# A message-passing layer on one core: blocks 26 to 103 go singly in TensorE's order, sums are placed later, and a softmax rests four turns

## Chip, core and metric

One core of a Trainium2 chip. The metric is the device time of one execution in microseconds: 1315.15 us for the kernel before, the median of three runs (1313.95 to 1321.31).

## What is computed

A graph layer over 8192 nodes with 256 features and 131072 edges sorted by destination, all in float32. `bn` is a scale and a shift per feature. The layer:

```
ea  = edge_attr @ w_e + b_e                       # 64 -> 256 features per edge
msg = relu(x[src] + ea)
agg = segment_sum(msg, dst)                       # over the edges of a node
h_local = bn(relu((x + agg) @ w1 + b1) @ w2 + b2 + x)
# attention inside groups of 32 consecutive nodes, 4 heads of 64
q, k, v = split(x @ in_w.T + in_b)
o = softmax(q k^T / 8) v
h_attn = bn(o @ out_w.T + out_b + x)
out = h_local + h_attn
out = bn(out + relu(out @ m_w1 + m_b1) @ m_w2 + m_b2)
result = layernorm(x + out)
```

## The kernel before

Two kinds of work share the core. **Edge work** goes over 128 blocks of 1024 edges. **Node work** goes over 16 chunks of 512 nodes (attention, then the dense layers once the chunk's sums are complete).

One block of edges takes these steps. The names are those of the profile; L numbers are lines of the kernel before.

- `gather(b)` (L152 to 163): eight indirect DMAs on GpSimd's queue fetch x rows of 128 edges each into a tile `xs`, of which there are four buffers. Blocks 0 to 19 read x itself, later ones `xb`, a copy of x with the edge bias added, which the kernel writes during the first blocks (`copy_load`, `copy_stream`, `copy_some`: loads and stores on SyncE's queue, adds on VectorE, L621).
- `load_edges`, `edge_transpose`, joined in `next_edges`: SyncE loads edge features, VectorE transposes them (L190).
- `edge_products(b)`: TensorE multiplies them by w_e (L208) into two PSUM tiles `pe`. For blocks under 20 it also adds the bias by a matmul (L203).
- `edge_messages(b)`: VectorE adds `xs` (L229, two adds a block), which frees the block's `xs` buffer; ScalarE applies the relu (L233).
- `edge_hot(b)`: VectorE builds a 0/1 matrix `oh` that sends each edge to one of 32 rows (L241).
- `edge_sums(blocks)`: TensorE multiplies it by the messages (L255) into one PSUM bank `pw`; ScalarE copies this to `ws` (L265); VectorE builds a second 0/1 matrix `oh2` (L269). It takes one block or two.
- `edge_place(blocks, ws, oh2)`: TensorE multiplies `ws` by `oh2` (L280), in the same bank under the name `l2`, and VectorE adds the window to the chunk's transposed nodes `xT` (L289).

Node work is written as generators that yield the planned cost, in microseconds, of the TensorE work that they have just issued. `attention_front` loads and transposes x (L434) and makes q and k (L445); `attention_back` makes v (L459) and the scores (L476, in the tiles `pe`), the softmax, its product with v (L514) and the output projection (L526); `dense` holds the four dense layers (L545), a transpose back (L582), the norm and the store. Four streams (BACK, FRONT, DENSE, DENSE2) hold these generators. `Work.run(us)` (L651) takes steps from the streams in turn until the planned costs reach `us`. A call of `run` is a turn: a generator that yields `REST` goes on in the second turn after the one in which it stopped, one that yields `PAUSE` in the next. If no stream may go, the rest of the amount is dropped down to 2 us.

The order on TensorE is the order of the program, written out by hand. On VectorE and ScalarE it is also stated for blocks below `NV` = 26 (`stated[0]`), and set by a scheduler of the language after that. Three parts follow each other in the main loop:

- blocks 0 to 103 (`TAIL` = 104), in pairs (L739 to 779). A pair issues, in this order: both gathers (two blocks ahead), products and messages of b, the sums of the pair before, products and messages of b + 1, the placing of those sums, and node work in three or four calls of `run` between these, `per` in all: 2 x 4.2 us for blocks under 20, 2 x 5.1 us later. Below 26 the calls are 0.3, then the place, 0.2 and 0.5; from 26 on they are 0.2, 0.1, then the place, 0.2, the `edge_hot` of both blocks, 0.5.
- blocks 104 to 127 (L781 to 825): a planner with a clock of its own takes the next step by due times. `came` holds the planned arrival of each block's gather, `added` that of its messages, and `work.step` fills the time until the next due step with node work.
- `work.finish()`, whatever is left.

Of the kernel before, what the change touches and what calls it, by code (L numbers as in the profile page):

```python
# [40 lines left out]
NV = 26  # L41
TAIL = 104
# [4 lines left out]
REST = -1.0  # L47
# [13 lines left out]
def first_node(b):  # L61
    return b * NPB - SLACK[b]
# [10 lines left out]
def gnn_kernel(ctx: ExitStack, tc: tile.TileContext, x, src, dst, edge_attr, w, out):  # L73
# [78 lines left out]
    def gather(b):  # L152
        xs = epool.tile([P, NH, TJ, C], FP, name="xs", tag="xs", bufs=4)
        for h in range(NH):
            for j in range(TJ):
                idx = srcd[:, b * NH + h, j : j + 1] if b < ND else srci[:, b, h * TJ + j : h * TJ + j + 1]
                nc.gpsimd.indirect_dma_start(  # L157
                    out=xs[:, h, j, :],
                    out_offset=None,
                    in_=x if b < NX else xb[:, :],  # L160
                    in_offset=bass.IndirectOffsetOnAxis(ap=idx, axis=0),
                )
        xs_of[b] = xs
# [19 lines left out]
    def between():  # L183
        for do in spots:
            do()
# [27 lines left out]
    def next_edges(b):  # L213
        if b < NB:
            edge_transpose(b)
        if b + 2 < NB:
            load_edges(b + 2)
# [18 lines left out]
    def edge_hot(b):  # L236

        oh = oh_of[b] = epool.tile([P, TB, WN], FP, name="oh", tag="oh", bufs=2)
        for t0 in range(0, TB, TB // 2):
            ts = slice(t0, t0 + TB // 2)  # L240
            nc.vector.tensor_tensor(  # L241
                oh[:, ts],
                iota_n[:, None, :WN].to_broadcast([P, TB // 2, WN]),
                rel[:, b, ts, None].to_broadcast([P, TB // 2, WN]),
                ALU.is_equal,
            )
# [45 lines left out]
    stated = [True]  # L292
# [336 lines left out]
    def copy_some(n=1):  # L629
        for _ in range(n):  # L630
            next(copying[0], None)

    class Work:
# [17 lines left out]
        def run(self, us):  # L651
            self.owed += us
            n = len(self.streams)
            self.rest = [max(r - 1, 0) for r in self.rest]
            while self.owed > 0:
                turns = [i % n for i in range(self.turn, self.turn + n)]
                i = next((i for i in turns if self.may(i)), None)
                if i is None:
                    break
                t = next(self.streams[i][0][1], None)  # L660
                if t is None:
                    self.streams[i].pop(0)
                elif t in (REST, PAUSE):
                    self.rest[i] = 2 if t == REST else 1
                else:
                    self.owed -= t
                    self.turn = (i + 1) % n
                    if t > 0:
                        between()
            self.owed = min(self.owed, 2.0)  # L670
# [24 lines left out]
    work = Work(4)  # L695
    PER = 5.1
    PER_X = 4.2
    OTHER = ("vn", "qk", "oT", "pr", "o")
    placed = -1
    with tc.manual_schedule(engines={PE}):  # L700

        def last_of(c, t_z=TN):

            return max(b for b in range(NB) if first_node(b) < c * CH + t_z * P)

        def summed(c, t_z=TN):
            last = last_of(c, t_z)
            return lambda: placed >= last and chunk[c].get("done") and not xp_of and b > 2

        for c in range(NCH):  # L710
            st, before, same = chunk[c], chunk[c - 1], chunk[c - 4]
            front = attention_front(c * CH, st, npool, bank)
            if c < 2:
                next(front)
            work.add(
                FRONT,
                lambda c=c, b=before, s=same: (c < 1 or b.get("scores"))
                and (c < 4 or s.get("dense")),
                front,
            )  # L720
            work.add(BACK, lambda s=st: s.get("front"), attention_back(st, npool, bank, bank2))
            if c < NCH - 2:
                work.add(DENSE, summed(c), dense(c * CH, st, npool, bank))
        for i, c, t_a, t_z in (
            (DENSE2, NCH - 2, 0, 2), (DENSE, NCH - 2, 2, 4), (DENSE2, NCH - 1, 0, 2), (DENSE, NCH - 1, 2, 3),
            (DENSE2, NCH - 1, 3, 4),
        ):
            d = dense(c * CH, chunk[c], npool, bank, t_a, t_z, *([OTHER] if i == DENSE2 else []))
            ready = summed(c, t_z)
            if i == DENSE2:  # L730
                ready = lambda r=ready: r() and chunk[NCH - 1].get("done")
            work.add(i, ready, d)

        spots.append(copy_some)
        early = ExitStack()
        early.enter_context(tc.manual_schedule(engines={mybir.EngineType.DVE, mybir.EngineType.Activation}))
        sums, waiting = None, []
        b = 0
        while b < TAIL:  # L739
            if b == NV:  # L740
                early.close()
                stated[0] = False
            blocks, per = range(b, b + 2), 2 * (PER_X if b < NX else PER)
            copying[0] = copy_stream(b // 2 - 1)
            for i in blocks:
                if i + 2 < NB:
                    gather(i + 2)
                if 4 <= i < 8:
                    wt, name = ((w1, "w1"), (w2, "w2"), (mw1, "m_w1"), (mw2, "m_w2"))[i - 4]
                    nc.sync.dma_start(wt, w[name].rearrange("(k p) m -> p k m", p=P))  # L750

            if b:
                edge_products(b)
                edge_messages(b)
                next_edges(b + 2)
            if waiting:
                sums = edge_sums(waiting)
            waiting = list(blocks)
            if not stated[0]:
                work.run(0.2 * per)  # L760
            edge_products(b + 1)
            edge_messages(b + 1)
            next_edges(b + 3)
            if stated[0]:
                for i in blocks:
                    edge_hot(i)
                    copy_some(2)
            work.run((0.3 if stated[0] else 0.1) * per)
            copy_load(b // 2)
            if sums:  # L770
                edge_place(*sums)
                placed, sums = sums[0][-1], None
            work.run(0.2 * per)
            if not stated[0]:
                for i in blocks:
                    edge_hot(i)
            work.run(0.5 * per)
            copy_some(4 * TN)
            b += 2

        came = [7.9 + 10.035 * (i + 1) for i in range(NB)]  # L781
        t, p, m, s, l = came[b - 2] + 20, b, b, b - 2, b - 2
        added = dict((i, came[i] + 2.0) for i in range(b))
        summed_at, bank_free = {}, t
        work.at = [t] * len(work.streams)
        while l < NB:

            times = [1e9] * 4
            if l < s:
                times[0] = summed_at[l] + 1.5  # L790
            elif s < m:
                times[1] = max(added[s] + 1.2, bank_free)
            if p < NB and m == p:
                times[2] = added[p - 1]
            if m < p:
                times[3] = came[m]
            if t >= times[0]:
                edge_place(*sums)
                placed = l
                t += 0.75  # L800
                bank_free = work.placed_at = t + 0.7
                l += 1
            elif t >= times[1]:
                sums = edge_sums([s])
                t += 1.2
                summed_at[s] = t
                s += 1
            elif t >= times[2]:
                if p + 2 < NB:
                    gather(p + 2)  # L810
                edge_products(p)
                next_edges(p + 2)
                edge_hot(p)
                t += 2.1
                p += 1
            elif t >= times[3]:

                with ExitStack() as behind:
                    for i in newest.values():
                        behind.enter_context(tc.issue_after(i))  # L820
                    edge_messages(m)
                added[m] = max(t, came[m], added[m - 1] + 0.5) + 2.0
                m += 1
            elif l == s - 1 == NB - 1:
                t = times[0]
            else:
                t = work.step(t, min(times))
        work.finish()
# [124 lines left out]
```

## Time and profile before

| | us |
|---|---|
| median of three runs | 1315.15 |
| the profiled execution, its own time | 1315.3 |
| span of its profile | 1313.3 |
| TensorE's matmuls busy | 1196.5 (91%) |
| GpSimd busy | 976.1 (74%) |
| VectorE busy | 800.9 (61%) |
| ScalarE busy | 589.2 (45%) |

Busy times are shares of one span and do not add up, as the engines work side by side. PE is TensorE's matmuls, PEld its weight loads, DVE VectorE, ACT ScalarE, POOL GpSimd, SP SyncE; a q behind the name is the engine's queue. A row with "x864 | 820.7, 950 | 263.4 <-issue 245.1" reads: 864 instructions, busy 820.7 us in all, 950 ns each, and 263.4 us in which the engine was idle just before them, 245.1 of it with no cause that the profile shows ("issue"). A row of a stretch gives its bounds, its length, each engine's busy time with the number of instructions, the granted TensorE clock (1 is full), the share of time in which the DMA engines were busy, and GB/s. A row of the chain or of the timeline begins with the start and the length in us.

### The profile page before, as it was taken

What the parts mean: (1) busy time and instruction counts of PE and PEld (TensorE: products, weight loads), DVE (VectorE), ACT (ScalarE), POOL (GpSimd) and SP (SyncE); (2) the same over time, 40 slices, a digit from 0 to 9 for tenths busy, and PEclk for the clock granted to TensorE, in tenths of its full rate; (3) what the DMA queues carried; (4) which work ended last, traced back from release to release, by engine and by line L of the source; (5) the groups of instructions that cost most, each with busy time, mean ns of one, the idle gap of its engine ahead of it and who ended that gap; (6) DMA issues with size and microseconds to landing.
All of it is one profiled execution on the core that took longest, in us unless ns stands there. A gap on an engine that the chain in (4) does not pass through costs nothing.

```text
span 1313.3 us, 20960 instructions
## 1 busy us (share of the span) xinstructions
PE 1196.5 (91%) x7635; PEld 720.4 (55%) x7635; DVE 800.9 (61%) x1629; ACT 589.2 (45%) x841; POOL 976.1 (74%) x1032
## 2 busy tenths in 40 slices
PE   4987989999999989898997998989898999989987
PEld 3554655556555655554554554545556555555655
DVE  5567665756666565745646574565647558475754
ACT  2524443454545363544544444353454445444433
POOL 6777777777777777777777777777777777777772
PEclk8988999999999989998998998989898999999989
DMA  9999876677766665755757566576567567655742
GB/s 234 283 338 273 263 210 175 172 183 193 177 170 170 169 183 162 195 155 157 194 157 185 154 185 168 154 186 170 170 169 189 149 169 193 162 162 161 193 129 58
DMA packets 148905, 240.34 MB, mean 183 GB/s; under 512 B 27934, under 2 KB 112188, under 8 KB 148028
## 3 DMA queue, kind: packets, MB, share of 16 engines
q0 software_dynamic: 49152, 134.28, 38.0%
q1 hardware_dynamic: 98556, 104.65, 29.5%
q8 instruction: 62, 1.02, 0.3%
q14 instruction: 47, 0.39, 0.1%
q10 hardware_dynamic: 1088, 0.00, 0.0%
HBM read 222.06 MB, written 16.78 MB: 182 GB/s over the span
## 4 chain that ended last, share of the span: by engine, by line
PE 49%; POOL 20%; issue 10%; DMA 9%; DVE 7%; ACT 4%; SPq 0%; DVEq 0%; POOLq 0%; ACTq 0%
POOL xs L157 20%; PE at L545 13%; PE pe L208 10%; PE at L445 6%; DMA xs<-xb,srci 5%; PE pw L255 5%; PE at L526 3%; PE l L280 3%; PE pe L203 2%; DVE msg L229 2%; PE at L459 2%; DMA xs<-in_x_dram,srci 2%; PE at L514 1%; ACT pr L486 1%; DVE bd L506 1%
## 5 line engine op out<-in xcount | busy, mean ns | idle before, releaser
L157 POOL DMA_INDIRECT xs<-xb,srci x864 | 820.7, 950 | 263.4 <-issue 245.1
L233 ACT ACTIVATE msg<-msg 128x1024 f32<-128x1024 f32 (+1 forms) x259 | 270.0, 1046 | 402.6 <-DVE msg L229 398.6
L229 DVE TENSOR_TENSOR msg<-pe,xs 128x1024 f32<-128x1024 f32 (+1 forms) x259 | 306.5, 1205 | 196.0 <-PE pe L208 75.8
L208 PE MATMUL pe<-we,eaT 64*128 64x256 f32 x2048 | 267.8, 398 | 17.0 <-ACT pr L486 11.8
L208 PEld LDWEIGHTS pe<-we,eaT 64*128 64x128 f32 x2048 | 193.6, 192 | 121.2 <-issue 62.7
L157 POOL DMA_INDIRECT xs<-in_x_dram,srci x144 | 138.3, 961 | 43.9 <-issue 39.9
L255 PE MATMUL pw<-msg,oh 128*32 128x256 f32 x2048 | 128.8, 384 | 1.4 <-ACT msg L233 1.0
L545 PE MATMUL at<-hA,mw 128*128 128x512 f32 (+2 forms) x304 | 124.8, 538 | 3.4 <-DVE hA L555 3.4
L445 PE MATMUL at<-xT,inT 128*128 128x512 f32 x256 | 121.9, 602 | 3.2 <-ACT xT L435 3.2
L545 PE MATMUL at<-m,mw 128*128 128x512 f32 (+2 forms) x304 | 119.0, 534 | 0.1
L190 DVE STREAM_TRANSPOSE eaT<-ea 128x512 f32<-128x512 f32 x128 | 89.9, 702 | 24.7 <-PE pe L208 20.7
L255 PEld LDWEIGHTS pw<-msg,oh 128*32 128x32 f32 x2048 | 59.5, 110 | 63.3 <-issue 22.9
L280 PEld LDWEIGHTS l<-oh,ws 128*128 128x128 f32 x512 | 74.4, 196 | 28.1 <-issue 20.9
L280 PE MATMUL l<-oh,ws 128*128 128x160 f32 (+4 forms) x512 | 86.3, 309 | 2.4 <-ACT ws L265 1.6
L545 PEld LDWEIGHTS at<-hA,mw 128*128 128x128 f32 x304 | 54.1, 192 | 51.6 <-issue 40.8
L545 PEld LDWEIGHTS at<-m,mw 128*128 128x128 f32 x304 | 54.6, 192 | 48.7 <-issue 44.9
L445 PEld LDWEIGHTS at<-xT,inT 128*128 128x128 f32 x256 | 46.9, 191 | 57.5 <-issue 48.3
L448 ACT ACTIVATE qk<-at,vec 128x512 f32<-128x512 f32 x64 | 43.9, 685 | 74.9 <-PE at L445 74.8
L545 PE MATMUL at<-xT,w 128*128 128x512 f32 (+2 forms) x152 | 68.5, 588 | 7.4 <-DVE xT L289 7.4
L545 PE MATMUL at<-h,w 128*128 128x512 f32 (+2 forms) x152 | 65.0, 550 | 9.6 <-ACT oT L521 6.3
L561 ACT ACTIVATE m<-at,vec 128x512 f32<-128x512 f32 (+2 forms) x76 | 46.8, 618 | 56.5 <-PE at L545 56.2
L570 DVE SCALAR_TENSOR_TENSOR zT<-at,s,zT 128x512 f32<-128x512 f32 (+2 forms) x38 | 25.1, 662 | 72.0 <-PE at L545 72.0
(113 smaller groups left out, 1228.3 us busy)
## 6 DMA issues: line engine op xcount, KB each, us to landing
ea<-in_edge_attr_dram SPq DMA_DIRECT2D x512, 128.0 KB
xs<-xb,srci POOLq DMA_INDIRECT x864
xn<-in_x_dram SPq DMA_DIRECT2D x16, 512.0 KB
out_dram<-y SPq DMA_DIRECT2D x14, 512.0 KB
xp<-in_x_dram SPq DMA_DIRECT2D x10, 512.0 KB
xb<-xp SPq DMA_DIRECT2D x10, 512.0 KB
xp<-in_x_dram SPq DMA_DIRECT2D x3, 1024.0 KB
xb<-xp SPq DMA_DIRECT2D x3, 1024.0 KB
```

The lines of the kernel that those rows point to most:

```text
L157: nc.gpsimd.indirect_dma_start(out=xs[:, h, j, :], out_offset=None, in_=x if b < NX else xb[:, :], in_offset=bass.IndirectOffsetOnAxis(ap= ...
L190: nc.vector.transpose(eaT, ea[:, QR:].rearrange("p (g d) -> p g d", d=ED)[:, :, :QR])
L208: nc.tensor.matmul(pe[:, i, u, :], eaT[rows, h + u], we[rows, :], start=(b >= NX), stop=True, skip_group_check=True)
L229: nc.vector.tensor_add(msg[:, hs, js].rearrange("p u i c -> p i u c"), pe[:, js, u : u + n, :], xs[:, hs, js].rearrange("p u i c -> p i u c"),
L233: nc.scalar.activation(msg[:, hs, js], msg[:, hs, js], AF.Relu)
L255: nc.tensor.matmul(pw[h * WN : (h + 1) * WN, i, :], oh[:, h * TJ + j, :], msg[:, h, j, :], start=(j == 0), stop=(j == TJ - 1), skip_group_ ...
L280: nc.tensor.matmul(l2[:, k, at : at + wn], ws[:, i, k * P : (k + 1) * P], oh2[:, i, :wn], start=(i == 0 and k == 0), stop=(i == last), ski ...
L445: nc.tensor.matmul(ps, inT[:, k, o * P : (o + 1) * P], xT[:, k, :], start=(k == 0), stop=(k == KC - 1))
L448: nc.scalar.activation(qk[:, o, :], ps, AF.Identity, bias=v_("in_b", o))
L526: nc.tensor.matmul(ps, outT[:, k, o * P : (o + 1) * P], oT[:, k, :], start=(k == 0), stop=(k == KC - 1))
L545: nc.tensor.matmul(ps, wt[:, k, o * P : (o + 1) * P], act[:, k, :], start=(k == 0), stop=(k == nk - 1))
L561: nc.scalar.activation(m1[:, o, :], layer(mw1, KC, o, hA), AF.Relu, bias=v_("m_b1", o))
```

## The change

Blocks 0 to 25 stay in pairs, but the place of the sums is followed by one call of `run` with 0.7 of the pair's amount instead of two with 0.2 and 0.5. From block 26 to 103 the loop takes one block at a time: products and messages of b, the sums of b - 1 alone, `run` with 0.4 of the block's amount, `edge_hot(b)`, 0.3, the place of b - 1, 0.3. From block 26 on, a generator that yields `REST` goes on in the fourth turn after it instead of the second. The planner starts at block 104 with one block still to be summed instead of two. Everything else is the same.

```diff
@@ Work.run
                 elif t in (REST, PAUSE):
-                    self.rest[i] = 2 if t == REST else 1
+                    self.rest[i] = (2 if stated[0] else 4) if t == REST else 1
@@ main loop
-        while b < TAIL:
-            if b == NV:
-                early.close()
-                stated[0] = False
+        while b < NV:
             blocks, per = range(b, b + 2), 2 * (PER_X if b < NX else PER)
             copying[0] = copy_stream(b // 2 - 1)
             for i in blocks:
...
             if waiting:
                 sums = edge_sums(waiting)
             waiting = list(blocks)
-            if not stated[0]:
-                work.run(0.2 * per)
             edge_products(b + 1)
             edge_messages(b + 1)
             next_edges(b + 3)
-            if stated[0]:
-                for i in blocks:
-                    edge_hot(i)
-                    copy_some(2)
-            work.run((0.3 if stated[0] else 0.1) * per)
+            for i in blocks:
+                edge_hot(i)
+                copy_some(2)
+            work.run(0.3 * per)
             copy_load(b // 2)
             if sums:
                 edge_place(*sums)
                 placed, sums = sums[0][-1], None
-            work.run(0.2 * per)
-            if not stated[0]:
-                for i in blocks:
-                    edge_hot(i)
-            work.run(0.5 * per)
+            work.run(0.7 * per)
             copy_some(4 * TN)
             b += 2
 
+        early.close()
+        stated[0] = False
+        for b in range(NV, TAIL):
+            gather(b + 2)
+            edge_products(b)
+            edge_messages(b)
+            next_edges(b + 2)
+            sums = edge_sums(waiting)
+            waiting = [b]
+            work.run(0.4 * PER)
+            edge_hot(b)
+            work.run(0.3 * PER)
+            edge_place(*sums)
+            placed = sums[0][-1]
+            work.run(0.3 * PER)
+        b = TAIL
+
         came = [7.9 + 10.035 * (i + 1) for i in range(NB)]
-        t, p, m, s, l = came[b - 2] + 20, b, b, b - 2, b - 2
+        t, p, m, s, l = came[b - 2] + 20, b, b, b - 1, b - 1
```

## What the change was predicted to do

> **What bounds the kernel now.** I read four views: the page's first part, then GpSimd's gather line by itself, then the chain of waits at the end, then counts of gathers and message adds by stretch. The page first.
>
> ```profile
> span 1313.3 us, 20960 instructions
> PE 1196.5 (91%) x7635; PEld 720.4 (55%) x7635; DVE 800.9 (61%) x1629; ACT 589.2 (45%) x841; POOL 976.1 (74%) x1032
> ```
>
> By busy time TensorE looks like the bound. The next views say otherwise: the gather line (minimum/median/maximum duration in ns, first and last start in us), GpSimd's own waits (total, times, longest), and GpSimd in order of time near the end.
>
> ```profile
> L157 POOL DMA_INDIRECT xs<-xb,srci x864: 942/948/1072, 207.4 to 1290.2; - x173
> L157 POOL DMA_INDIRECT xs<-in_x_dram,srcd x16: 942/948/1402, 4.2 to 23.9; - x16
> ...
> POOL xs L157 <- issue: 292.2, 951, 2.6
> POOL xs L157 <- DMA xs<-xb,srci: 5.8, 19, 0.3
> ...
> 1270.15 0.95 POOL L157 DMA_INDIRECT xs<-xb,srci  x1 [0.30 <-issue]
> 1290.23 0.95 POOL L157 DMA_INDIRECT xs<-xb,srci  x1 [0.30 <-issue]
> ```
>
> There are 1024 gathers, 8 to a block. The last 863 steps take (1290.2 - 207.4) / 863 = 1.2547 us each, and the sixteen steps up to the last one 20.08 / 16 = 1.255: one pace from start to end, 0.95 of work and 0.30 of issue, though GpSimd counts as only 74% busy. No wait for data is longer than 0.3 us, which is the ordinary issue gap. So GpSimd never stops: from 4.2 to 1291.2 us it issues gathers, one block every 8 x 1.2547 = **10.04 us**. The first 160 took (207.4 - 4.2) / 160 = 1.270 us each, 2.4 us more in all than at the later pace. This is all that any new order could win from the gathers. Now what follows the last of them (the chain of waits: start, length, what).
>
> ```profile
> 1291.22 0.68 DVE msg L229
> ...
> 1297.49 6.12 PE at L545 x52
> 1303.61 0.40 PE at L582 x2
> 1304.01 2.75 PE at L545 x24
> ...
> 1309.22 0.41 DVE y L595
> ```
>
> The tail from 1291.2 to 1313.3 us is 22.1 us: last messages, last sums, the last 128 rows' dense layers, norm and store. The kernel's time is gathers plus tail; TensorE's order counts only where it stops a gather or lengthens the tail.
>
> An order could stop a gather through the four xs buffers (L153): block b+4 may not be gathered before block b's message adds (L229) are done. So I counted both by stretch: first the adds (2 a block), then the gathers (8 a block); behind them, the tightest place, from VectorE's and GpSimd's timelines.
>
> ```profile
> 0.00:187.00 187.00, 36.52 (x30) 0.94 0.95 271
> 294.00:462.00 168.00, 42.51 (x36) 0.98 0.68 177
> ...
> 0.00:187.00 187.00, 139.13 (x144) 0.94 0.95 271
> 294.00:462.00 168.00, 127.26 (x134) 0.98 0.68 177
> ...
> 185.70 1.22 DVE L229 TENSOR_TENSOR msg<-pe,xs 128x1024 f32<-128x1024 f32 x1 [0.50 <-PE pe L208]
> 187.28 0.95 POOL L157 DMA_INDIRECT xs<-in_x_dram,srci  x1 [0.30 <-DVE xp L621]
> ```
>
> By 187.0 us 144 gathers (blocks 0 to 17) and 30 adds (blocks 0 to 14) are done. The gather at 187.28 is the first of block 18; it takes block 14's buffer, whose last add ended at 185.70 + 1.22 = 186.92. **0.36 us to spare.** Later there is room: from 294 to 462 us 36 adds, 18 blocks, go by in 168 us, 9.33 us a block against GpSimd's 10.04. TensorE gains 0.71 us a block until it meets the gathers:
>
> ```profile
> DVE msg L229 <- DMA xs<-xb,srci: 53.8, 27, 5.0
> ...
> 1260.14 2.88 DMA xs<-xb,srci
> ```
>
> From 294 to 1040 us the adds wait 27 times for gathered rows to land, up to 5.0 us. There TensorE's side waits for GpSimd. So the profile holds two reserves: buffers (about 27 us where the adds follow the landing at once: three blocks of 10.04, less 2.88 for a landing, the second row) and 0.71 us a block of speed.
>
> **The change part by part.** Its own counts come from the order in which the two programs stand on each engine, which holds no times; durations are from these rows (mean ns of one; a TensorE instruction leaves two rows, a transpose at L434 one).
>
> ```profile
> L445 PE MATMUL at<-xT,inT 128*128 128x512 f32 x256 | 121.9, 602 | 3.2 <-ACT xT L435 3.2
> L514 PE MATMUL at<-bd,vn 128*64 128x128 f32 x512 | 35.4, 297 | 13.6 <-DVE bd L506 13.6
> L434 PE MATMUL at<-ident,xn 128*128 128x128 f32 x128 | 18.9, 290 | 6.9 <-ACT oT L521 4.1 <-ACT h L552 2.8
> L459 PE MATMUL at<-inT,xT 128*128 128x256 f32 x256 | 61.3, 382 | 0.5 <-ACT m L561 0.5
> L255 PE MATMUL pw<-msg,oh 128*32 128x256 f32 x2048 | 128.8, 384 | 1.4 <-ACT msg L233 1.0 <-DVE xT L289 0.4
> ```
>
> *GpSimd's queue:* the same instructions in the same order. Cost 0.
>
> *The pairs up to block 25, and the rests.* The last two runs of a pair are joined, so a pair has two turns instead of three and a rest of two turns lasts a whole pair. Node work moves back. Ahead of block 14's products, the tight place, stand eight 512-wide matmuls, 16 of L514 and 8 transposes fewer. A 512-wide one costs 121.9 / 128 = 0.952 us, one of L514 35.4 / 256 = 0.138, a transpose 18.9 / 128 = 0.148: 7.6 + 2.2 + 1.2 = 11.0 us less. The adds of block 14 come up to 11 us earlier, and the spare 0.36 us becomes up to 11. It saves no time, since no gather had been stopped there. At block 26 eight 512-wide ones are still owed, 7.6 us.
>
> *Single blocks, 26 to 103.* TensorE's matmuls are the same in number and shape; only their order differs. At block 104 the owed work is six 512-wide and four 256-wide matmuls (61.3 / 128 = 0.479 us each): 5.7 + 1.9 = 7.6 us, as at block 26, so the stage neither gains nor loses. At every block from 10 to 120 the new order has less node work ahead of the products than the old one, by 1 to 14 us; against it stand at most one sum (128.8 / 128 = 1.0 us) and one or two places that come earlier. So a block's products, and the adds that free the gather's buffer, are not later through the amount of work ahead.
>
> *Sums placed later and singly.* VectorE and ScalarE get new operations, priced by the same shapes in the trace:
>
> ```profile
> L289 DVE TENSOR_TENSOR xT<-l,xT 128x448 f32<-128x448 f32 x20 | 12.0, 599 | 3.9 <-PE l L280 3.9
> L289 DVE TENSOR_TENSOR xT<-l,xT 128x352 f32<-128x352 f32 x21 | 10.6, 506 | 1.1 <-PE l L280 1.0
> L289 DVE TENSOR_TENSOR xT<-l,xT 128x320 f32<-128x320 f32 x2 | 1.0, 484 | 0.0
> L289 DVE TENSOR_TENSOR xT<-l,xT 128x224 f32<-128x224 f32 x6 | 2.3, 389 | 4.5 <-PE l L280 4.5
> L265 ACT COPY ws<-pw 128x512 f32<-128x512 f32 x51 | 29.0, 569 | 0.1
> L265 ACT COPY ws<-pw 128x256 f32<-128x256 f32 x25 | 9.3, 372 | 33.9 <-PE pw L255 33.7
> L496 ACT ACT_TABLE_LOAD  x10: 1283/1283/1283, 324.4 to 1154.2; - x10
> ```
>
> VectorE: 20 adds of 448 and 18 of 352 elements (12.0 + 9.1 = 21.1 us) become 58 of 320 and 18 of 224 (28.1 + 7.0 = 35.1): 14 us more over 78 blocks, 0.18 a block. ScalarE: 38 copies of 569 ns become 76 of 372, 6.7 us more, and four table loads, 5.1 us: 0.15 a block. VectorE's idle 39% and ScalarE's 55% hide both, so I take 0. Without that cover 0.33 us a block would still lie inside the 0.71 of reserve.
>
> The place now waits behind 0.7 x 5.1 = 3.6 us of planned node work for a 0.37 us copy (before: 0.3 of a pair, 3.1 us); the next sums wait for one add of 0.48 us behind 1.5 us of node work and the next products. If VectorE is late with that add, the next sums, node work and products queue on TensorE. I bound this unseen wait from 0 (its slot is longer than the copy and the add) to 1.6 us a block, 14.2 / 9 from the nearest wait of this kind:
>
> ```profile
> PE pe L476 <- DVE msg L229: 14.2, 9, 2.7
> ```
>
> I take 0, which is nearer to the rows of sums and places (L255 above waited 1.4 us in the whole run). A small gain is as possible, and equally without effect.
>
> *The tail.* At block 121 four transposes are owed (0.6 us), from block 124 on nothing. TensorE's last 172, VectorE's last 72 and ScalarE's last 47 instructions are the same in the same order. Cost 0.
>
> **Sum.** 1315.3 us (the profiled execution's own time, 2.0 outside its span; the median shown is 1315.15) + 0 on gathers + 0 on the tail: **1315.0 us**, between the two.
>
> [...] The clock by stretch first (TensorE's busy time leads; the granted clock is third from the end).
>
> ```profile
> 294.00:462.00 168.00, 162.04 (x1048) 97.91 (x1044) 107.06 (x212) 77.59 (x105) 127.26 (x134) 0.98 0.68 177
> 1000.00:1060.00 60.00, 53.48 (x345) 32.51 (x344) 36.68 (x74) 31.16 (x43) 45.51 (x48) 0.91 0.62 169
> ```
>
> The 9.33 us a block hold at a clock of 0.98; at the 0.91 of 1000 to 1060 us they would be 9.33 x 0.98 / 0.91 = 10.05, no reserve left. [...] I take no effect: a pause for rows comes only where TensorE is ahead.
>
> **The rivals.**
>
> *New waits make TensorE the bound (slower).* Place: blocks 26 to 103, the sums waiting for VectorE's add. It decides from 0.71 us of new wait a block. At 1.58 us: (1.58 - 0.71) x 78 = 68 us behind, less up to 27 us of buffers: 41 us of stopped gathers, **1356 us**. For it: VectorE must empty one shared bank twice as often. Against: the slots above, and 7.6 us less work ahead. Chance 0.08.
>
> *The clock falls (slower).* Single blocks spread the pauses; from a clock of 0.91 on the reserve is gone. At 0.87 a block takes 9.33 x 0.98 / 0.87 = 10.51 us, 0.47 x 78 = 37 us less 27: **1325 us**. Against: falling behind itself ends the pauses. Chance 0.02.
>
> *Block 20's gather waits for the copy of x (slower).* It starts at 207.4 us and needs the last xb store, issued at
>
> ```profile
> 195.26 0.38 SPq L623 DMA_DIRECT2D xb<-xp  x1
> ```
>
> One pair later, 20 us, it would start at about 215, some 8 us late: **1323 us**. But the last copies stand in the same pair as before, and that pair comes earlier. Chance 0.01.
>
> *Tail and early gathers shrink (faster).* If all but the last 128 rows' 24 matmuls (48 rows of the 76 shown at L545) left the tail, 28 x 8.87 / 76 = 3.3 us would go; with the 2.4 us of the slow early gathers: **1309.6 us**. The equal last orders speak against the first part. Chance 0.03.
>
> *The change does nothing that counts:* it is my forecast, chance 0.86. The order does change (from block 5 on), so "not done" is excluded.
>
> **How the numbers follow.** A measurement of this kernel can tell about 0.5%, 6.6 us, from no change. Faster by more needs a time under 1308.6, which even the full gain above (1309.6) does not reach without scatter: 0.02. Slower: 0.08 + 0.02 + 0.01 = 0.11. Within: the rest, 0.87. The range: the forecast less the 2.4 us of early gathers, 1312; upward 1320, as single runs of before reach 1321.3. It holds about 0.8 of the 0.86; the slow rivals are left out.
>
> **What would show it.** Right: gathers still 1.2547 us apart from 207 us on, no wait for data over 0.3 us, a tail of 22 us, block 14's last add about 10 us ahead of block 18's first gather, some 38 more adds at L289's place. Wrong: a GpSimd wait on the message adds of microseconds, the last gather starting after 1292, or TensorE waits at the sums above 55 us in all.

## The result, and the profile after

The changed kernel took **1321.73 us** (median of 19 runs, 1319.37 to 1323.8) against 1315.63 us for the kernel before, measured beside it (19 runs, 1313.95 to 1321.31): a ratio of **1.0035, 95% interval 1.0026 to 1.0044**. It is slower by a third of a per cent. That is less than the 0.5% which the prediction called "within", but it is measured, and 1.7 us above the upper end of the range.

The profiled execution took 1322.21 us with a span of 1320.4 us, 7.1 us more than the span before. The first part of its page:

```profile
span 1320.4 us, 21136 instructions
PE 1203.0 (91%) x7635; PEld 713.7 (54%) x7635; DVE 812.3 (62%) x1667; ACT 590.4 (45%) x883; POOL 975.2 (74%) x1032
```

VectorE has 1667 - 1629 = 38 instructions more, as counted from the order; TensorE has the same number and is busy 6.5 us longer.

The gather line of the changed kernel, with GpSimd's own waits (total, times, longest):

```profile
L157 POOL DMA_INDIRECT xs<-xb,srci x864: 942/946/1430, 207.8 to 1289.2; - x173
...
POOL xs L157 <- issue: 293.6, 956, 2.7
POOL xs L157 <- DVE msg L229: 4.9, 16, 0.3
```

The gathers still run from end to end without a stop: (1289.2 - 207.8) / 863 = 1.2531 us each, and no wait for data longer than the ordinary 0.3 us. The last one even starts 1.0 us earlier than before. So the 7.1 us, and one more, lie behind the gathers. The chain of waits at the end of the changed kernel:

```profile
1293.54 0.68 DVE msg L229
...
1297.08 2.01 PE pw L255 x16
...
1299.76 1.18 PE l L280 x4
...
1301.34 8.66 PE at L545 x52
...
1315.60 0.41 DVE y L595
```

and two of the same steps in the kernel before:

```profile
1294.57 1.15 PE pw L255 x16
...
1296.39 0.70 PE l L280 x4
```

Set beside the same steps of before, the 7.1 us split in three:

- **The last messages are 2.3 us later**: 1293.54 against 1291.22.
- **The same TensorE work takes 4.1 us longer.** From the messages to the group of 52 it is 1301.34 - 1293.54 = 7.80 us against 6.27, and the group takes 8.66 against 6.12. The last sums (L255) take 2.01 against 1.15, the last placing (L280) 1.18 against 0.70.
- **The last store ends 0.7 us later** after the last y: 1320.4 - 1315.60 = 4.8 against 1313.3 - 1309.22 = 4.1.

The clock by stretch in the changed kernel shows what the middle part is (bounds, length, TensorE's busy time and instructions, granted clock):

```profile
1296.00:1298.00 2.00, 2.00 (x16) 0.64 0.07 16
1298.00:1300.00 2.00, 1.21 (x13) 0.50 0.38 123
...
1302.00:1304.00 2.00, 2.00 (x11) 0.50 0.00 0
...
1306.00:1308.00 2.00, 2.00 (x16) 0.80 0.00 0
```

From 1298 to 1306 us, 8 us, TensorE runs at half its clock (0.50 granted); in the profile of before the clock is 1.00 in all six stretches from 1296 to 1308:

```profile
1302.00:1304.00 2.00, 2.00 (x19) 1.00 0.00 0
```

Why the last messages are late is read from the blocks that the planner orders. The stretch from the first products of block 104 to those of block 122, TensorE alone, before:

```profile
1064.80:1239.30 174.50, 163.84 (x1054) 0.99 0.65 172
```

and after:

```profile
1055.50:1243.00 187.50, 171.99 (x1050) 0.97 0.63 169
```

The changed kernel reaches block 104 9.3 us earlier and block 122 3.7 us later. It was ahead at 104 because it did less node work on the way: in blocks 26 to 103 TensorE's side waits for rows still more than before (77.6 us against 53.8 from 294 to 1040 us):

```profile
DVE msg L229 <- DMA xs<-xb,srci: 77.6, 47, 3.5
```

In the planner's stretch it then has 8.2 us more busy time and 187.5 - 172.0 = 15.5 us of idle time against 10.7. Towards its end the kernel before has caught up with the gathers: from 1180 to 1291 us its adds wait for rows again,

```profile
DVE msg L229 <- DMA xs<-xb,srci: 5.2, 3, 2.0
```

and in the changed kernel they do not wait for rows once in that time. The longest idle time of TensorE in the changed kernel's stretch is this one (its timeline; the bracket holds the idle time ahead and what ended it):

```profile
1180.48 3.62 PE L514 MATMUL at<-bd,vn 128*64 128x128 f32 x32 [4.35 <-DVE bd L506]
```

and the clock behind it:

```profile
1180.00:1184.00 4.00, 3.52 (x32) 0.57 0.81 181
```

TensorE stands 4.35 us for a softmax. From 1180 to 1184 us the granted clock is 0.57, and the 32 rows of matmuls behind the pause take 3.62 us; in the kernel before, 32 rows of the same kind took 1.97:

```profile
1102.17 1.97 PE L514 MATMUL at<-bd,vn 128*64 128x128 f32 x32
```

### The profile page after: what moved, and what is told of

It is laid out like the page before. It is cut to its first block, busy times and chain, and to the rows that moved or that the text cites. A ratio compares the mean times of both kernels' runs of the same rounds, so it can differ in the third digit from the quotient of the medians.

```text
span 1320.4 us, 21136 instructions
## 1 busy us (share of the span) xinstructions
PE 1203.0 (91%) x7635; PEld 713.7 (54%) x7635; DVE 812.3 (62%) x1667; ACT 590.4 (45%) x883; POOL 975.2 (74%) x1032
## 3 DMA queue, kind: packets, MB, share of 16 engines
q10 hardware_dynamic: 1088, 0.00, 0.0%
## 4 chain that ended last, share of the span: by engine, by line
PE 50%; POOL 16%; DVE 11%; DMA 10%; issue 10%; ACT 3%; DVEq 0%; SPq 0%; ACTq 0%; POOLq 0%
PE at L545 16%; POOL xs L157 16%; PE pe L208 10%; PE at L445 6%; DMA xs<-xb,srci 5%; PE pw L255 5%; DVE msg L229 3%; PE l L280 3%; PE at L526 3%; PE at L514 2%; PE pe L203 2%; DMA xs<-in_x_dram,srci 2%; DVE bd L506 1%; PE at L459 1%; PE at L434 1%
## 5 line engine op out<-in xcount | busy, mean ns | idle before, releaser
L255 PE MATMUL pw<-msg,oh 128*32 128x256 f32 x2048 | 142.5, 398 | 13.1 <-DVE xT L289 9.3
L545 PE MATMUL at<-hA,mw 128*128 128x512 f32 (+2 forms) x304 | 128.9, 549 | 11.0 <-DVE hA L555 10.8
L255 PEld LDWEIGHTS pw<-msg,oh 128*32 128x32 f32 x2048 | 56.9, 112 | 85.7 <-issue 35.7
L289 DVE TENSOR_TENSOR xT<-l,xT 128x320 f32<-128x320 f32 (+11 forms) x145 | 57.0, 410 | 73.3 <-PE l L280 73.0
L280 PEld LDWEIGHTS l<-oh,ws 128*128 128x128 f32 x512 | 77.8, 192 | 44.5 <-issue 33.2
L280 PE MATMUL l<-oh,ws 128*128 128x160 f32 (+4 forms) x512 | 88.7, 300 | 2.9 <-ACT ws L265 2.1
L241 DVE TENSOR_TENSOR oh<-iota_n,rel 128x128 f32<-128x128 f32 x256 | 59.7, 273 | 17.7 <-PE pw L255 17.7
```

The source lines that it names most:

```text
L241: nc.vector.tensor_tensor(oh[:, ts], iota_n[:, None, :WN].to_broadcast([P, TB // 2, WN]), rel[:, b, ts, None].to_broadcast([P, TB // 2, WN ...
L255: nc.tensor.matmul(pw[h * WN : (h + 1) * WN, i, :], oh[:, h * TJ + j, :], msg[:, h, j, :], start=(j == 0), stop=(j == TJ - 1), skip_group_ ...
L280: nc.tensor.matmul(l2[:, k, at : at + wn], ws[:, i, k * P : (k + 1) * P], oh2[:, i, :wn], start=(i == 0 and k == 0), stop=(i == last), ski ...
L289: newest["xT"] = nc.vector.tensor_add(xT, l2[:, :, a - n : z - n], xT).ins
L545: nc.tensor.matmul(ps, wt[:, k, o * P : (o + 1) * P], act[:, k, :], start=(k == 0), stop=(k == nk - 1))
```

## The experiments

The theory was that work left over at block 104 comes back where TensorE has no time for it. The rivals: the single blocks themselves, the longer rest, the clock at the end, and the order that the planner happens to make after block 104. Ratios are to the kernel before, measured beside each kernel, with 95% intervals.

### Four kernels on a chip that ran slower

The first four ran on a chip on which the kernel before took 2018.14 us (median of 17). The edits, the first to the kernel before, the others to the changed kernel:

```diff
# early pairs joined, pairs throughout
+            if stated[0]:
+                work.run(0.7 * per)
+            else:
+                work.run(0.2 * per)
...
# single blocks alone
-                    self.rest[i] = (2 if stated[0] else 4) if t == REST else 1
+                    self.rest[i] = (2 if stated[0] else 2) if t == REST else 1
-            work.run(0.7 * per)
+            work.run(0.2 * per)
+            work.run(0.5 * per)
# rest of two
+                    self.rest[i] = 2 if t == REST else 1
# catching up
-            work.run(0.3 * PER)
+            work.run(0.3 * PER + (1.7 if 90 <= b < 94 else 0.0))
```

Early pairs joined, nothing else:

> The kernel before with one part of the change alone: below block 26 the two last runs of a pair are joined, so a pair has two turns; pairs stay from block 26 on. By the order of the program 7.4 us of node work are owed at block 104, as in the changed kernel. Theory L (node work put off early is never made up before block 104, TensorE waits for gathers meanwhile, and the last blocks' messages come late): as slow as the changed kernel, 1319 to 1322 us, last message adds about 2 us later than before's 1291.2. Rival S (the single blocks cost the time, by more sums, places and waits): 1315 to 1316.5 us. Rival C (nothing but the clock that happens to be granted at the end): between, with scatter.

Measured: 2024.67 us, 1.0011 [0.9972, 1.0051].

Single blocks alone, with the early pairs and the rest of before:

> The changed kernel with the early pairs as before (three turns) and a rest of two turns: single blocks from 26 to 103 alone. Nothing is owed at block 104 (0.0 us). Theory L: 1315 to 1316.5 us, last message adds near 1291.2. Rival S: 1319 to 1322 us. Rival C: scatter between.

Measured: 1952.79 us, 0.9671 [0.9616, 0.9726].

The changed kernel with a rest of two:

> The changed kernel with a rest of two turns throughout. 7.4 us are owed at block 104 and 2.8 at 121 (changed kernel 7.5 and 0.9). Theory L: as slow as the changed kernel or a little slower, 1320 to 1323 us. Rival R (the longer rest is what costs): 1315 to 1316.5 us. Rival S: 1319 to 1322 us.

Measured: 1922.43 us, 0.9527 [0.9475, 0.9578].

The changed kernel that catches up in blocks 90 to 93:

> The changed kernel with 1.7 us of node work more planned in each of the blocks 90 to 93, a stage in which its TensorE waits for gathers; what is owed falls from 9.5 to 1.9 us at block 94 and to -0.2 at 104. Theory L: the loss goes, 1315 to 1317 us, last message adds near 1291.2. Rival S: nothing changes, 1319 to 1322 us. Rival C: scatter between.

Measured: 1933.2 us, 0.959 [0.9528, 0.9651].

None of the four tells the theories apart, for one reason. GpSimd's waits in the second of them, with a span of 1950.5 us:

```profile
POOL xs L157 <- DVE msg L229: 550.2, 75, 19.5
```

The gathers stop 75 times for the message adds, up to 19.5 us, which they never did in the profile of before, and the three kernels with single blocks are 3 to 5% faster. This says nothing of the 0.35%, so all four were measured again on other chips, the first and the last at once.

### The same two where the gathers set the pace

> The same kernel as e1_early_only (pairs throughout, the early pairs with two turns), since there every kernel, the one before too, took half as long again as before. On a chip where the kernel before takes 1315 us, theory L (the node work put off early, 7.4 us at block 104, makes the last messages late): 1319 to 1322 us, last message adds about 2 us later than 1291.2. Rival S (single blocks cost the time): 1315 to 1316.5 us.

Measured: 1327.79 us (1325.72 to 1328.6), 1.0091 [1.0073, 1.0108]. The early pairs alone cost more than the whole change, and more than theory L allowed. Its chain:

```profile
1299.23 0.68 DVE msg L229
...
1306.73 7.43 PE at L545 x52
```

> The same kernel as e4_catchup90 (the changed kernel with 1.7 us more planned node work in each of blocks 90 to 93, nothing owed at block 104), for the same reason. Theory L: 1315 to 1317 us, last message adds near 1291.2. Rival S: 1319 to 1322 us.

Measured: 1320.26 us (1316.54 to 1322.57), 1.0031 [1.0018, 1.0045]. Catching up late brings next to nothing, against theory L. The stretch from block 104's products to block 122's in its profile:

```profile
1062.60:1243.10 180.50, 166.43 (x1036) 0.96 0.64 169
```

Block 104 starts 7.1 us later than in the changed kernel, as the work is done ahead of it, and block 122 at the same time.

### The clock at the end, and single blocks alone

Eight matmuls whose result nobody reads were put into the gaps of the last steps, in the changed kernel, in the kernel before and with single blocks alone; a fourth kernel is single blocks alone as above.

```diff
+    def warm(n):
+        d = bank()
+        for _ in range(n):
+            nc.tensor.matmul(d[:, :P], ident, ident, start=True, stop=True)
...
+        if blocks[-1] == NB - 1:
+            warm(2)
...
+        if blocks[-1] == NB - 1:
+            warm(1)
...
+            if o == KC - 1 and nt == 1 and t_a == 2:
+                warm(2)
...
+                warm(3)
```

> The changed kernel with eight idle matmuls of 128 columns (identity by identity into a spare bank, read by nobody) in the four gaps of TensorE's tail: two behind the last chunk's first dense layer, three behind its second, two behind the last sums, one behind the last place. Theory K (4.2 us of the loss is TensorE at half its clock during the last 80 matmuls, since the gaps before them lower the clock): 1317 to 1319 us, the 52 matmuls at the first dense line in 6.1 us again as in the kernel before, not 8.66, no run above 1320. Rival (the loss is lateness alone): 1320 to 1324 us as before, or up to 2 us more for the added matmuls.

Measured: 1320.21 us (1318.17 to 1323.78), 1.0041 [1.0025, 1.0056]. In its profile (whose line numbers are 5 to 9 higher) the end runs at full clock (1.00 from 1291 to 1311 us), and the messages are late all the same:

```profile
1294.29 0.68 DVE msg L234
...
1300.56 6.12 PE at L554 x52
```

> The kernel before with the same eight idle matmuls. Theory K: its runs of 1319 to 1321 us (8 of 36 so far) go, median 1314 to 1316 us. Rival: the median grows by up to 2 us and the upper runs stay.

Measured: 1314.99 us (1314.13 to 1316.86), 0.999 [0.9979, 1.0002]. (Of the 36 runs named, 7 lay above 1319 us, not 8.)

> The same kernel as e2_singles_alone (single blocks from 26 to 103, early pairs with three turns and a rest of two turns as before; nothing owed at block 104). Theory L (node work put off in the early pairs is the cause): 1313 to 1316.5 us. Rival S (single blocks cost the time): 1319 to 1322 us. Rival P (the order that the planner of blocks 104 to 127 happens to make decides, by its waits on softmax and sums): no fixed number; TensorE idle between the products of blocks 104 and 122 above before's 10 us where it is slower, below where it is faster.

Measured: 1315.6 us (1313.73 to 1319.7), 1.0004 [0.9993, 1.0015]. With the order that the planner makes here, **single blocks cost nothing that these runs can tell**, and their last messages are on time:

```profile
1291.71 0.68 DVE msg L229
...
1297.99 6.12 PE at L545 x52
```

> g3_singles_alone with the eight idle matmuls in the tail. Theory K: no run in the upper group, spread under 4 us, median at or up to 2 us under that of g3_singles_alone; with theory L 1313 to 1316 us, at least as fast as the kernel before.

Measured: 1315.53 us (1313.78 to 1317.06), 0.9999 [0.999, 1.0007].

The extra matmuls do not move a median. Of before, 3 of 31 runs lay at 1320.1 to 1320.8 us and with them none of 12 above 1316.9; that is too few to show that they take single high runs away. In the changed kernel, runs of 1322 to 1323.8 stayed. So the half clock at the end explains 4 us of one profile, and not the ratio.

### Repaying the work that was left over

The first and the second have a rest of two, the third is the changed kernel, the fourth is single blocks alone with a rest of three. The edits to the changed kernel:

```diff
# repaid in blocks 60 to 63, and 2 for the rest
+            work.run(0.3 * PER + (1.7 if 60 <= b < 64 else 0.0))
# repaid in blocks 100 to 103
+            work.run(0.3 * PER + (1.7 if 100 <= b < 104 else 0.0))
# single blocks, 3 for the rest, early pairs as before
+                    self.rest[i] = (2 if stated[0] else 3) if t == REST else 1
```

> The changed kernel with a rest of two turns and 1.7 us more planned node work in each of blocks 60 to 63: the early pairs have two turns as in the change, but nothing is owed from block 64 to 103 (0.0 to 1.9 us), and the planner of blocks 104 to 127 makes an order close to that of g3_singles_alone. Theory L (what is still owed when TensorE begins to wait for gathers is lost): 1314 to 1317 us. Theory P (the planner's order after block 104 decides): 1314 to 1317 us too. Rival E (the early pairs with two turns cost of themselves, whatever is owed later): 1319 us or more.

Measured: 1317.72 us (1315.51 to 1321.45), 1.0019 [1.001, 1.0029], between the forecasts.

> The same kernel as e3_rest2 (the changed kernel with a rest of two turns, 7.4 us owed at block 104 and 2.8 at 121), on the usual chip. Theory L: 1319 to 1324 us, last message adds after 1293. Rival R (the longer rest is what costs): 1315 to 1316.5 us.

Measured: 1324.3 us (1323.15 to 1328.29), 1.0074 [1.0061, 1.0087]. Its chain, at full clock (1.00 from 1281 to 1316 us):

```profile
1298.86 0.68 DVE msg L229
...
1305.13 6.12 PE at L545 x52
```

> The changed kernel with 1.7 us more planned node work in each of blocks 100 to 103. 8.1 us are owed at block 100 and -0.2 at 104; from 104 on TensorE's order is the same as in f4_catchup90, which took 1320.3. Theory P: as f4_catchup90, 1318 to 1321 us. Theory L with idle lost before block 100: as slow as the changed kernel, 1320 to 1323 us; it should then be slower than f4_catchup90, which repaid ten blocks earlier.

Measured: 1318.72 us (1317.04 to 1323.0), 1.0028 [1.0018, 1.0039].

> g3_singles_alone with a rest of three turns from block 26 on: early pairs as before, nothing owed at 104, a third order of the planner. Theory L: 1314 to 1317 us. Theory P: anything from 1314 to 1321, by the order; if it is as fast as g3 with another order, order alone is not the cause.

Measured: 1318.88 us (1316.39 to 1323.32), 1.0035 [1.0023, 1.0048].

With 7.4 us owed at block 104, by the planned costs, and a rest of two, the last messages are 1298.86 - 1291.22 = 7.6 us late; repaid in blocks 60 to 63, where TensorE's side waits for rows anyway, most of the loss is gone (1.0074 to 1.0019). But the amount is not the whole of it. The changed kernel owes 7.5 us at block 104 and its last messages are only 2.3 us late. Its adds still wait for rows in blocks 90 to 103 (916 to 1055 us of its profile):

```profile
DVE msg L229 <- DMA xs<-xb,srci: 17.9, 11, 2.9
```

and repaying there gave back next to nothing (1.0031 and 1.0028 against 1.0035). The last kernel owes nothing and loses 0.35% too. Something else is of the same size.

### The planner's order alone

One line more at the start of the planner moves the pointer to the stream whose turn it is. Gathers, blocks 0 to 103 and the work left at 104 stay the same; only the order of node work behind that point changes: in the kernel before, TensorE's order differs from 1067 to 1088 us of the profile and is the same ahead of that and behind it. It was put into the kernel repaid in blocks 100 to 103 (3), into single blocks alone (2) and into the kernel before (2).

```diff
         work.at = [t] * len(work.streams)
+        work.turn = (work.turn + 2) % 4
```

> The changed kernel with the owed work repaid in blocks 100 to 103 (the kernel that took 1.0028), and one line more: at the start of the planner the pointer to the stream whose turn it is moves back by one. Nothing else differs: not the gathers, not the work that is left at block 104, not the order before it. Theory P (the 0.3% that stays without owed work comes from the order that the planner happens to make after block 104): the ratio moves by more than 0.1%, in either direction; back to 1.0000 to 1.0015 if another order is a better one, with the last messages at 1291.2 to 1292.5 us. Rival R (the loss comes from how blocks 26 to 103 go: the longer rest, or the pairs before 26): the ratio stays at 1.0018 to 1.0039 and the last messages start at 1293.4 to 1294.8.

Measured: 1316.96 us (1314.41 to 1320.52), 1.001 [0.9998, 1.0023]; the same kernel without the line had 1.0028 [1.0018, 1.0039]. The last messages in the two profiles, first without the line, then with it:

```profile
1294.73 0.68 DVE msg L229
```

```profile
1291.47 0.68 DVE msg L229
...
1299.16 8.78 PE at L545 x52
```

They are on time again, as theory P had it. The profiled run with the line took 1320.08 us all the same, as its group of 52 matmul rows took 8.78 us.

> Single blocks alone (early pairs with three turns, rest of two; 1.0004), and one line more: at the start of the planner the pointer to the stream whose turn it is moves by two, which gives another order of node work after block 104. Theory P: the ratio moves away from 1.0004 by more than 0.1%, most likely upward, to 1.0015 to 1.004, with the last messages 1 to 3 us later than 1291.7. Rival R: it stays within 0.9993 to 1.0015.

Measured: 1318.82 us (1314.6 to 1322.19), 1.0016 [1.0001, 1.0031]; without the line 1.0004 [0.9993, 1.0015]. The intervals overlap, so this pair alone shows no move; its last messages start at 1293.56 us, 1.85 later than without the line.

> The kernel before, and one line more: at the start of the planner the pointer to the stream whose turn it is moves by two. Only some dozen runs of node work between blocks 104 and 110 change places. Theory P: a small move or none, 0.999 to 1.002, since the order is the old one again within about five blocks. Rival R: 1.000.

Measured: 1320.6 us (1316.34 to 1326.17), **1.0034 [1.0021, 1.0047]**, more than I had expected. One line that changes TensorE's order over some 20 us, near blocks 104 to 106, makes the kernel before as slow as the changed one. The profile (of its longest run, 1326.17 us) shows how. TensorE's longest wait from 1064 to 1291 us, in its timeline:

```profile
1103.89 3.79 PE L208 MATMUL pe<-we,eaT 64*128 64x256 f32 x16 [6.07 <-DVE msg L229]
```

The clock around it, and the last messages in the chain:

```profile
1100.00:1104.00 4.00, 0.11 (x2) 0.89 0.63 197
1104.00:1108.00 4.00, 4.00 (x20) 0.50 0.72 214
```

```profile
1298.04 0.68 DVE msg L229
```

A block's products stand 6.07 us for the message adds of the block before, and run at half clock (0.50) behind it. The same block in the kernel before:

```profile
1098.96 2.26 PE L208 MATMUL pe<-we,eaT 64*128 64x256 f32 x16 [1.64 <-DVE msg L229]
```

What kept the adds is on VectorE's timeline of the turned kernel:

```profile
1095.10 1.28 DVE L585 TENSOR_TENSOR y<-at,xn 128x512 f32<-128x512 f32 x2
...
1098.59 2.14 DVE L506 STREAM_TRANSPOSE bd<-pr 32x512 f32<-32x512 f32 x3
...
1101.19 1.51 DVE L595 TENSOR_SCALAR y<-y,mv,rstd 128x256 f32<-128x256 f32 x4
1102.63 2.34 DVE L229 TENSOR_TENSOR msg<-pe,xs 128x1024 f32<-128x1024 f32 x2
```

A softmax (up to L506) and a norm (L585 to L595) have met on VectorE, and the adds at 1102.63 come behind both. In the changed kernel a softmax and a norm met too, ahead of the wait of 4.35 us, but mostly on ScalarE (its timeline):

```profile
1172.87 0.30 ACT L590 ACTIVATE rstd<-mv,eps_t 128x4 f32<-128x4 f32 x1
1173.19 1.28 ACT L496 ACT_TABLE_LOAD   x1
1174.48 0.63 ACT L496 ACTIVATE pr<-pr 128x512 f32<-128x512 f32 x1
```

VectorE had the softmax ready for its exponential (L496) at 1173.06 us, but ScalarE was at the norm's `rstd` and then loaded a table in 1.28 us; the exponential began 1.4 us later. The rest of the 4.35 us is not ascribed.

## Why the prediction was wrong

**What held.** GpSimd's gathers set the pace and were never stopped: same queue, same pace, no wait for data above 0.3 us. Block 14's adds came earlier, as forecast: they end at 172.94 + 2.35 = 175.29, the gather that takes their buffer starts at 187.71, so 12.4 us to spare, where "about 10" was forecast (VectorE's and GpSimd's timelines):

```profile
172.94 2.35 DVE L229 TENSOR_TENSOR msg<-pe,xs 128x1024 f32<-128x1024 f32 x2
...
187.71 0.95 POOL L157 DMA_INDIRECT xs<-in_x_dram,srci  x1 [0.30 <-DVE bd L506]
```

The new sums and places stopped no gather either: 13.1 us of waiting at the sums in the whole run, against the 55 that would have spoken for that rival, and a ratio of 1.0004 when the single blocks are alone (1.0016 with the pointer moved).

```profile
L255 PE MATMUL pw<-msg,oh 128*32 128x256 f32 x2048 | 142.5, 398 | 13.1 <-DVE xT L289 9.3
```

**What failed** is the step "*The tail.* At block 121 four transposes are owed (0.6 us), from block 124 on nothing. [...] Cost 0." It took the last instructions, which are equal, for the whole tail, and so priced blocks 104 to 123 at nothing. The sum's term "+ 0 on the tail" was 8.1 us in the profile, less 1.0 us on the gathers; 4.1 us of it is the half clock at the end of this one profile (the medians differ by 6.1 us). Three things bear on it:

- *The order behind block 104 has a price of its own.* Shown for the kernel before: one line that changes it costs 0.34%. For the changed kernel it is likely: with the owed work repaid in blocks 100 to 103 it still lost 0.28%, and another order behind that brought it to 0.10%. How an order costs is seen in single profiles: TensorE stood 6.07 us where message adds came behind a softmax and a norm on VectorE, and 4.35 us for a softmax that a norm had held up by 1.4 us on ScalarE. The prediction compared amounts of work ahead of a block, not what meets on VectorE and ScalarE.
- *"7.6 us, as at block 26, so the stage neither gains nor loses"* was true of blocks 26 to 103 and of no use. TensorE's side passed blocks 26 to 103 with more waiting for rows (77.6 us against 53.8) and did the owed work behind block 104, where there is little of it: in the kernel before no add waits for rows from 980 to 1180 us. Joining the early pairs alone cost 0.91%, and with single blocks and a rest of two 0.74%, of which repaying at 60 to 63 gave back 0.55%. Late by 7.6 us with 7.4 us owed speaks for the amount as the cause, but each of these edits changes the planner's order as well, 7.5 us owed made the changed kernel only 2.3 us late, and repaying in blocks 90 to 103 gave back no more than 0.07%. The share of each in the changed kernel's 0.35% is not separated. That the rest of four wins back half of the 0.74% may itself be the order.
- *The clock: "I take no effect: a pause for rows comes only where TensorE is ahead".* The prediction's two stretches had the clock at 0.98 with TensorE busy 162.04 of 168 us, and at 0.91 with 53.48 of 60. The pauses that count are not for rows: 4.35 us for a softmax, with a granted clock of 0.57 from 1180 to 1184 us and 3.62 - 1.97 = 1.65 us more for the matmuls behind it, and in the turned kernel 6.07 us for message adds, with 0.50 over the 4 us behind it. At the end of the kernel the clock fell to 0.50 with no pause near that length: the longest in the 10 us ahead of it was 0.83 us.

No rival had the place: those that were slower put their waits into blocks 20 to 103, where the new waits stopped no gather (9.3 us in the whole run at the sums for the add into `xT`, 0.4 before).

**Open.** The order is not only its longest wait. TensorE's longest wait from 1055 us on in the kernel repaid in blocks 100 to 103, which costs 0.28%, is

```profile
PE at L545 <- DVE xT L289: 5.0, 4, 3.3
```

and with the pointer moved, at a cost of 0.10%, it is longer:

```profile
PE at L514 <- DVE bd L506: 4.5, 1, 4.5
```

Which order is best was not found; none of these kernels beats the one before beyond its interval where the gathers set the pace. Runs of one and the same program also differ by as much as these kernels do, and with the clock: with single blocks alone, the three runs above 1318 us had mean granted clocks of 0.960 to 0.963, the nine others 0.966 to 0.972. So an order may cost by how often the clock falls, which these runs do not separate; the changed kernel as such had no lower clock (0.964 to 0.972 over its 19 runs) than the kernel before (0.954 to 0.969 in the runs beside the experiments).

## What to carry to other kernels

Where one engine's queue sets the pace, find the last stretch in which the other engines have no slack, and price the order there by itself: amounts of work may be equal while two bursts meet on a third engine. Work that is put off past the time that an engine spends waiting for data has to be done somewhere else: here repaying it in blocks 60 to 63 took the loss from 0.74% to 0.19%, though repaying it in blocks 90 to 103 did little. And when a change of a few tenths of a per cent is judged, run the old kernel with a harmless change of order as well: here that alone moved it by 0.34%.

## What the runs showed of the hardware

Two pauses of TensorE cost more than their length. After 6.07 us of standing still in the turned kernel the granted clock was 0.50 over the next 4 us, and the 16 rows of a block's products took 3.79 us, where they took 2.26 in the kernel before. After 4.35 us in the changed kernel it was 0.57 from 1180 to 1184 us, and 32 rows took 3.62 us, against 1.97 in the kernel before. Behind another it did not fall: in the kernel before TensorE stood 4.08 us up to 14.32 us, and the clock was 1.00 over the next 4 us.

At the end the half clock comes in some executions and not in others, from almost the same gaps. TensorE's timeline in the changed kernel, where the clock then fell to 0.50:

```profile
1294.20 0.94 PE L545 MATMUL at<-h,w 128*128 128x128 f32 x6 [0.64 <-ACT h L552]
1295.97 1.11 PE L545 MATMUL at<-hA,mw 128*128 128x128 f32 x4 [0.83 <-DVE hA L555]
```

and in the kernel before, where it stayed at 1.00:

```profile
1291.89 0.94 PE L545 MATMUL at<-h,w 128*128 128x128 f32 x6 [0.65 <-ACT h L552]
1293.74 0.83 PE L545 MATMUL at<-hA,mw 128*128 128x128 f32 x4 [0.91 <-DVE hA L555]
```

One chip ran the same program in 2018 us instead of 1315, with a mean granted clock of 0.82 to 0.83 against 0.95 to 0.97 on the others. With single blocks alone the profile there shows pauses at TensorE that it puts down to nothing, 62.6 us ahead of the matmuls of the placing (L280), where the page of the same kernel on another chip has 6.2 us idle ahead of them in all, 5.3 of it for ScalarE's copy (L265). The three kernels with single blocks were 3 to 5% faster than the one before on that chip, where the gathers of one of them stopped for 550.2 us behind message adds, and had ratios of 1.0004 to 1.0074 on the others: what set the pace was not the same there. Why it ran slower is open.
